# A transformer layer with attention and gated LoRA experts: activations transposed by VectorE and DRAM in place of TensorE, an earlier first product, and a plan whose transfers share one line

## The chip, the cores and the metric

The kernel runs on one core of one Trainium2 chip. The metric is the device time of one execution in microseconds (us), median of several runs, less being better.

## The reference

The input is x with 8 batches of 256 rows of 512 numbers, float32. All of it stays in float32.

```python
xn = (x - mean(x)) / sqrt(var(x) + 1e-5)               # per row
q, k, v = xn @ wq.T, xn @ wk.T, xn @ wv.T              # 32, 8 and 8 heads of 128
q, k = rope(q), rope(k)
scores = q @ k.T / sqrt(128)                           # 4 query heads share one key head
scores = scores * key_scale                            # 0.5 / 1.5 / 1.0 by key; rows from 107 on
probs = softmax(scores + causal_mask)
s = concat(probs @ v) @ wo.T
logits = xn @ router_w.T                               # 4 experts, the best 2 are kept
gates = softmax(top2(logits))
delta = sum_e gates_e * (xn @ A_e.T @ B_e.T) * 4       # rank 16
out = x + s * silu(delta)
```

## The kernel before

**Work and its parts.** Batches are taken in four pairs (`tb` 0 to 3), 512 rows or four tiles of 128 rows each. `norm(tb)` loads x, normalises it and puts the transposed activations into a tile `XB`; sums of its quarters go into `XT`. Both stand in a single buffer, so that a pair's `XB` can be written only when the last product of the pair before has read it.

All large products are done by Strassen's scheme with seven block products in place of eight. `quad` makes one projection of two times 256 output columns for a pair: `p1` and `p2` use parts of `XB`, `p6`, `p5`, `p7` and `p4` sums from `XT`, and `p3` `XB` again. Its PSUM banks are called `pa`, `pd` and `pe`, with a letter behind for queries, keys or values (`pak`, `pdq`). Each block product is eight matrix instructions of 128x256. The weight blocks and, from pair 1 on, their sums are fetched by GpSimd's queue into rings of nine and eight tiles; in pair 0 VectorE makes the sums and they are stored.

A step is one key head of a pair, `(tb, g)`; a unit is one batch of a step, so a step has two and the kernel 64, numbered 0 to 63. For each unit `softmax` computes scores (`sc`), exponentials and scaled probabilities; VectorE transposes them in blocks of 32 by 32 into `blocks`; SyncE stores them to DRAM with four transfers (`spread`, `there<-blocks`) and loads them with one (`gather`, `pT<-there`) in the order in which `values` needs them (`av<-pT,v`). `values` of a unit comes a step after its scores. `out_project` multiplies by the output weights and adds up seven sums in `acc` tiles. `put_together` combines them at the end of a pair, multiplies by the gates (`g`) and adds x (`xf`), which it loads with `inputs(0)` and `inputs(1)` into the two x buffers, 512 KB each, and stores the output. The last pair has its own version, `last_products`. `experts` computes router and gates from `XB` with `ra`, `bt` and `tab`.

**What sets the order.** A planner, `Plan`, runs through the whole kernel when it is built. Every piece of work is a job with an engine, an estimated time `takes`, jobs that it waits for (`after`), buffers that it opens and closes, and a `lag`: the time after its end until those behind it may start. TensorE's jobs get due times in the order in which they are laid; `run` derives the others' due times backwards from them, and then plays the kernel forward. Whenever an engine is free, the job due first, of those that are ready in that play, is issued. The instructions of each engine are put into the program in this order, and on the chip an engine keeps to it whatever the real durations are. A dependency that exists only in the plan makes an order, not a wait on the chip.

A transfer is a job whose `lag` is fixed: 6.0 us for a block of weights, 3.4 for the probabilities' stores behind 2.4 of issue, 7.0 for their gather behind 0.35 of issue, with `HOP` (0.18) for each step. Transfers do not hold each other up in the plan.

**The parts that the change touches.** In `norm`, for each tile: `load`, `statistics`, `variance`, `root`, `invert`, `normalise`, then `turn` (four TensorE transposes into a PSUM bank, `xp<-ident,xn`) and `read` (a copy by ACT into `XB`). The first pair's four turns are laid before the first products, `lay(norm(0))`, and its tables are loaded by `load_tables` on ACT's queue as one of the first jobs, beside the loads of x. From pair 1 on, the turns are laid between other products at the end of the step with g = 6.

Of the kernel before, what the change touches and what calls it, by code (L numbers as in the profile page):

```python
# [159 lines left out]
class Job:  # L160
# [3 lines left out]
    def __init__(self, engine, takes, what, after, opens, closes, near, lag, number):  # L164
        self.engine, self.takes, self.what, self.lag = engine, takes, what, lag
        self.opens, self.closes, self.near, self.number = opens, closes, near, number
        self.due, self.waits, self.then, self.started = float("inf"), len(after), [], False


class Plan:  # L170
# [4 lines left out]
    HOP = 0.18  # L175
    AHEAD = 30.0
# [4 lines left out]
    def add(self, engine, takes, what, after=(), opens=(), closes=(), near=None, lag=0.0):  # L181
        after = [a for a in after if a]
        job = Job(engine, takes, what, after, opens, closes, near, lag, len(self.jobs))
        for a in after:
            a.then.append(job)
        for hold in closes:
            hold.readers += 1
        self.jobs.append(job)
        return job

# [4 lines left out]
    def run(self):  # L195
        for job in reversed(self.jobs):
            if job.engine != "pe":
                if job.near:
                    job.due = job.near[0].due + job.near[0].takes + job.near[1]
                for after in job.then:  # L200
                    job.due = min(job.due, after.due - job.takes - job.lag - self.HOP)
        ready = {e: [] for e in ("pe", "dve", "act", "sp", "pool", "dma")}
        busy = dict.fromkeys(ready, 0.0)
        events, count = [], 0

        def offer(job):
            heapq.heappush(ready[job.engine], (job.due, job.number, job))

        for job in self.jobs:
            if not job.waits:  # L210
                offer(job)
        now, left = 0.0, len(self.jobs)
        laid = sorted((j for j in self.jobs if j.engine == "pe"), key=lambda j: -j.due)
        while left:
            while laid and laid[-1].started:
                laid.pop()
            limit = (laid[-1].due if laid else float("inf")) + self.AHEAD
            for engine, heap in ready.items():
                while heap and busy[engine] <= now:
                    tried, job = [], None  # L220
                    while heap:
                        entry = heapq.heappop(heap)
                        if entry[0] > limit:
                            tried.append(entry)
                            break
                        if all(h.room.has_for(h) for h in entry[2].opens):
                            job = entry[2]
                            break
                        tried.append(entry)
                    for entry in tried:  # L230
                        heapq.heappush(heap, entry)
                    if job is None:
                        break
                    for h in job.opens:
                        h.room.take()
                    job.started = True
                    job.what()
                    busy[engine] = now + job.takes
                    count += 1
                    heapq.heappush(events, (now + job.takes + self.HOP + job.lag, count, job))  # L240
                    heapq.heappush(events, (now + job.takes, -count, None))
            now, _, job = heapq.heappop(events)
            if job is None:
                continue
            left -= 1
            for h in job.closes:
                h.readers -= 1
                if not h.readers:
                    h.room.free += 1
            for after in job.then:  # L250
                after.waits -= 1
                if not after.waits:
                    offer(after)
# [3 lines left out]
def layer(ctx: ExitStack, tc: tile.TileContext, x, wquad, woquad, raT, bT, table, out):  # L257
# [14 lines left out]
    bounce = pool("bounce", 4, space=DRAM)  # L272
    store = pool("store", 1, space=DRAM)
# [31 lines left out]
    gates, sums_of, acts, weights, x_hold = {}, {}, {}, {}, {}  # L305
# [3 lines left out]
    def norm(tb):  # L309


        n = f"{tb}"
# [3 lines left out]
        ph = [hold("mm") for _ in range(NT)]  # L316
# [36 lines left out]

        def read(t):
            if t == 0:
                acts[tb] = (
                    one.tile([P, 2, NB, 2, S], F32, tag="XB", name=f"XB{tb}"),
                    one.tile([P, 4, 2, S], F32, tag="XT", name=f"XT{tb}"),
                )
            nc.scalar.copy(acts[tb][0][:, :, t // 2, :, bass.ts(t % 2, P)], box["p", t])  # L360

        def add_up(i):
            XB, XT = acts[tb]
            b11, b12, b21, b22 = XB[:, 0, 0], XB[:, 0, 1], XB[:, 1, 0], XB[:, 1, 1]
# [6 lines left out]
        for t in range(NT):  # L371
# [5 lines left out]
            add("dma", 0.0, lambda: None, after=[issues[t]], lag=8.5 if tb else 5.0 + 1.3 * t)  # L377
            for t in range(NT)
        ]
        sts = [add("dve", 0.9, lambda t=t: statistics(t), after=[loads[t]]) for t in range(NT)]  # L380
        begun.extend(issues)
        done = []

        for ts in [slice(0, NT)] if tb else [slice(t, t + 1) for t in range(NT)]:
            v = add("dve", 0.1, lambda ts=ts: variance(ts), after=sts[ts])
            r = add("act", 2.8 if tb else 0.2, lambda ts=ts: root(ts), after=[v])
            done += [add("dve", 0.1, lambda ts=ts: invert(ts), after=[r])] * len(sts[ts])
        reads, pieces = [], []
        for t in range(NT):
            xn = add("dve", 0.4, lambda t=t: normalise(t), after=[done[t]], opens=[mh[t]], closes=[xh[t // 2]])  # L390
            tp = add("pe", 0.5, lambda t=t: turn(t), after=[xn, identity], opens=[ph[t]], closes=[mh[t]])
# [11 lines left out]
        acts[tb, "B"], acts[tb, "T"] = reads, [t1, t2, t3, t4]  # L403
        return pieces
# [3 lines left out]
    def blocks_of(tb, room, ring, source, kept, key, form, first):  # L408
# [4 lines left out]
        order = (A11, A21, A22, A12, S1, S2, S4) if not tb else form.order  # L413
# [21 lines left out]
        if tb:  # L435
            for i in order:
                after = [sums_of[room, key, i]] if i in form.sums else []
                there[i] = add("pool", 0.8, lambda i=i: load(i), after=after, opens=[holds[i]], lag=6.0)
            return box, holds, there
        issue = list(first)  # L440
        for i in order[:4]:
            there[i] = add(
                "sp" if first else "pool", 0.4 if first else 0.8, lambda i=i: load(i), after=issue,
                opens=[holds[i]], lag=10.0 if first else 6.0,
# [6 lines left out]
        for i in form.sums:  # L451
            sums_of[room, key, i] = add(
                "pool", 0.8, lambda i=i: keep_sum(i), after=[there[i]], closes=[holds[i]],
                lag=5.0,
# [31 lines left out]
    def quad(tb, which, out, room, rows, name):  # L486
# [15 lines left out]
        def product(bank, i, half, b, t, first):  # L502
# [3 lines left out]
            xb = acts[tb][0][:, half, b] if t is None else acts[tb][1][:, t]  # L506
# [11 lines left out]
        def piece(bank, i, half, b, t, first, after):  # L518
            return add(
                "pe", 1.73, lambda: product(bank, i, half, b, t, first),  # L520
                after=[there[i]] + (XB if t is None else [XT[t]]) + after,
# [47 lines left out]
    def rope(src, of, dst, opens, after, name):  # L569
# [21 lines left out]
        def turn():  # L591
# [6 lines left out]
            after=after + [tables], opens=opens, closes=[of],  # L598
# [80 lines left out]
    free_p = [None]  # L679

    def softmax(tb, g, b):
# [119 lines left out]
        out_ = add("sp", 2.4, spread, after=[t1], closes=[bh], near=(sc, 5.0), lag=3.4)  # L801
        in_ = add("sp", 0.35, gather, after=[out_], opens=[th], lag=7.0)
# [116 lines left out]
    def last_products(n, abox, ah, a_done, wbox, wh, w_done):  # L919
# [18 lines left out]
        def load(what, b):  # L938
# [9 lines left out]
            loads[what, b] = add("sp", 0.3, work, after=after, opens=[hold(tag)], lag=9.0)  # L948
# [46 lines left out]
        def store(src, b, f, p, after, ts=slice(0, 2)):  # L995
# [3 lines left out]
                near=(p, 3.0), lag=4.0,  # L999
# [60 lines left out]
    def put_together(tb):  # L1060
# [15 lines left out]
        def inputs(b):  # L1076
# [4 lines left out]
            def load(what):  # L1081
# [4 lines left out]
            near = (M[2]["last"], -12.0)  # L1086
            done = [
                add("sp", 0.3, lambda: load("g"), after=gates[tb][2 * b : 2 * b + 2], opens=[xh],
                    near=near, lag=9.0),
                add("sp", 0.3, lambda: load("xf"), opens=[gh], near=near, lag=9.0),  # L1090
            ]
            loads[b] = box, [xh, gh], done

        def result(k, b, f):
# [17 lines left out]
                closes=[M[k]["hold"]], near=(near, 5.0), lag=4.0,  # L1112
# [18 lines left out]
    def experts(tb):  # L1131
# [5 lines left out]
        def route():  # L1137
            XB = acts[tb][0]
            lm = box["lm"] = ps_av.tile([P, NT, E + E * R], F32, tag="av", name=f"lm{n}")
            for t in range(NT):  # L1140
                for c in range(DC):
                    nc.tensor.matmul(
                        lm[:, t, :],
                        lhsT=XB[:, c // 2, t // 2, c % 2, bass.ts(t % 2, P)],
                        rhs=ra[:, c, :],
                        start=(c == 0),
                        stop=(c == DC - 1),
                    )
# [49 lines left out]
        p1 = add("pe", 3.75, route, after=acts[tb, "B"] + [tables], opens=[lh], closes=[x_hold[tb]])  # L1198
        r1 = add("dve", 2.0, rank_them, after=[p1], near=(p1, 2.0))
# [8 lines left out]
        def silu(t):  # L1208
# [15 lines left out]
            def whole():  # L1224
# [10 lines left out]
                    after=[d], closes=[h], near=(p, 4.0), lag=4.0,  # L1235
# [5 lines left out]
        return [p1], [p2], [[silu(t)] for t in range(NT)]  # L1241
# [41 lines left out]
    def load_tables():  # L1283
        nc.scalar.dma_start(out=tab, in_=table)
        nc.scalar.dma_start(out=ra, in_=raT.rearrange("(c p) m -> p c m", p=P))
        nc.scalar.dma_start(out=bt, in_=bT)

    identity = add("pool", 1.5, lambda: make_identity(tc.nc, ident), near=None)
    tables = add("act", 2.0, load_tables, lag=4.0)
# [8 lines left out]
    lay(norm(0))  # L1298
# [5 lines left out]
    lay(lead[:7] + route + lead[7:14] + turn + lead[14:])  # L1304

    for n in range(len(steps) + 2):
# [8 lines left out]
        if not last:  # L1315
# [7 lines left out]
            if tb + 1 < NTB and g == KV - 2:  # L1323
                turns = norm(tb + 1)
                for t in range(NT):
                    later[t] = later[t] + [turns[t]]
# [50 lines left out]
```

## Time and profile before

| | us |
|---|---|
| median of three runs | 1361.68 (1357.97, 1361.68, 1362.44) |
| profiled execution, its own time | 1358.35 |
| its span, first to last instruction | 1356.6 |
| TensorE busy | 1330.6 |
| VectorE busy | 1097.6 |
| ScalarE (ACT) busy | 618.5 |
| first large product starts | 14.02 |
| TensorE's waits for gathered probabilities | 9.4 in 6 waits |

The granted TensorE clock is 0.998 of full speed over the span. The DMA engines move 203 GB/s on average and are busy for 66% of the span. A line of a timeline has the start in us, the time in us, the engine, the line, the operation, out<-in by the program's names, and in brackets the idle time before and what ended it; a line of a list of waits has the total in us, how many times, and the longest. All instructions are recorded in a helper at line 118, so that they are told apart by their tiles. A q behind an engine's name is its queue of issues.

### The profile page before, as it was taken

The numbers are of one execution on the slowest core, as the hardware profiler recorded it, in microseconds if no ns is written. First come the engines' busy times: TensorE is split into PE (matmuls) and PEld (weight loads), VectorE is DVE, ScalarE is ACT, GpSimd is POOL, SyncE is SP. The second block draws the span as 40 slices with busy tenths as digits, with TensorE's granted clock in tenths as the row PEclk, the third lists the DMA queues.
The fourth block names the chain that finished last, engine by engine and source line by source line (L and its number), as shares of the span: only waits on it lengthen the run. The fifth ranks groups of instructions, "written<-read, shape, count | busy, mean of one in ns | idle before, by whom it ended". The sixth has DMA issues, their size and how long they took to land.

```text
span 1356.6 us, 19913 instructions
## 1 busy us (share of the span) xinstructions
PE 1330.6 (98%) x6512; PEld 1170.4 (86%) x6512; DVE 1097.6 (81%) x2827; ACT 618.5 (46%) x1590; POOL 314.1 (23%) x579
## 2 busy tenths in 40 slices
PE   7999999999999999999999999999999999999997
PEld 6888888888888888888888888888888988888986
DVE  5899989898888769689697875959868877676996
ACT  2465454453534435345453444435443455434621
POOL 2323222222222122221222122222122221222020
PEclk9999999999999999999999999999999999999999
DMA  5578766666766666676766666576676676565583
GB/s 172 180 250 256 216 186 223 217 212 207 242 177 212 207 197 185 202 226 181 215 200 217 200 213 202 171 226 206 178 227 193 197 219 202 188 198 186 156 282 106
DMA packets 106150, 275.81 MB, mean 203 GB/s; under 512 B 16000, under 2 KB 52864, under 8 KB 106048
## 3 DMA queue, kind: packets, MB, share of 16 engines
q0 software_dynamic: 45760, 149.98, 35.6%
q1 hardware_dynamic: 59536, 123.76, 29.9%
q8 instruction: 53, 0.87, 0.2%
q10 hardware_dynamic: 752, 0.80, 0.2%
q14 instruction: 49, 0.40, 0.1%
HBM read 194.79 MB, written 79.69 MB: 202 GB/s over the span
## 4 chain that ended last, share of the span: by engine, by line
PE 83%; DVE 9%; DMA 6%; issue 1%; ACT 1%; SPq 0%; DVEq 0%; ACTq 0%
PE po L118 23%; PE paq L118 14%; PE av L118 10%; PE sc L118 8%; PE pdq L118 7%; PE pak L118 4%; DMA pT<-there 4%; PE pav L118 4%; PE peq L118 3%; PE pdk L118 2%; DMA there<-blocks 2%; PE pdv L118 2%; DVE qTq L118 1%; DVE blocks L118 1%; DVE p L118 1%; DVE acc L118 1%
## 5 line engine op out<-in xcount | busy, mean ns | idle before, releaser
L118 ACT ACTIVATE p<-z,least 128x256 f32<-128x256 f32 (+7 forms) x512 | 207.6, 407 | 184.5 <-DVE least L118 137.0
L118 PE MATMUL po<-wo,a 128*128 128x256 f32 x992 | 233.3, 379 | 0.0
L118 PEld LDWEIGHTS po<-wo,a 128*128 128x128 f32 x992 | 186.4, 190 | 22.8
L118 PE MATMUL av<-pT,v 128*128 128x256 f32 x768 | 186.9, 383 | 9.4 <-DMA pT<-there 9.4
L118 DVE CUSTOM_DVE_ANT_0 z<-sc,tab 128x256 f32<-128x256 f32 (+7 forms) x512 | 134.0, 300 | 62.7 <-PE sc L118 59.3
L118 PE MATMUL paq<-XT,w 128*128 128x256 f32 x768 | 182.1, 380 | 0.3 <-ACT u3q L118 0.3
L118 PE MATMUL po<-wo,s 128*128 128x256 f32 x744 | 177.4, 381 | 0.2 <-PE av L118 0.2
L118 PEld LDWEIGHTS av<-pT,v 128*128 128x128 f32 x768 | 145.8, 192 | 30.8 <-issue 5.3
L118 PEld LDWEIGHTS sc<-kk,qTq 128*128 128x128 f32 x1024 | 159.0, 191 | 12.5 <-issue 0.8
L118 PE MATMUL sc<-kk,qTq 128*128 128x256 f32 (+7 forms) x1024 | 167.9, 302 | 0.1
L118 PEld LDWEIGHTS paq<-XT,w 128*128 128x128 f32 x768 | 144.9, 190 | 20.4 <-ACT u2q L118 0.8
L118 DVE TENSOR_TENSOR acc<-acc,po 128x512 f32<-128x512 f32 x189 | 128.2, 679 | 40.5 <-PE po L118 39.1
L118 POOL DMA_DIRECT2D w<-sums x144 | 78.9, 548 | 352.9 <-PE paq L118 158.7
L118 PEld LDWEIGHTS po<-wo,s 128*128 128x128 f32 x744 | 139.6, 190 | 23.7 <-issue 5.5
L118 ACT COPY a<-av 128x512 f32<-128x512 f32 x128 | 74.2, 580 | 179.6 <-PE av L118 179.2
L118 ACT COPY swq<-cq 64x1024 f32<-64x1024 f32 x128 | 133.7, 1045 | 15.0 <-DVE cq L118 10.7
L118 POOL DMA_DIRECT2D w<-in_wquad_dram x148 | 80.9, 548 | 244.9 <-PE paq L118 82.8
L118 DVE STREAM_TRANSPOSE blocks<-p 128x1024 f32<-128x1024 f32 (+1 forms) x128 | 123.6, 968 | 0.2
L118 DVE TENSOR_SCALAR p<-p,total 128x256 f32<-128x256 f32 (+7 forms) x512 | 117.1, 294 | 2.3
L118 DVE TENSOR_TENSOR qTq<-cq,tab 128x1024 f32<-128x1024 f32 x64 | 78.1, 1220 | 30.6 <-ACT cq L118 30.6
L118 ACT ACTIVATION_READ_ACCUMULATOR p<-z,least 128x1 f32 x512 | 95.8, 187 | 0.0
L118 POOL DMA_DIRECT2D wo<-in_woquad_dram x104 | 56.9, 548 | 128.4 <-PE po L118 118.5
(134 smaller groups left out, 1862.3 us busy)
## 6 DMA issues: line engine op xcount, KB each, us to landing
there<-blocks SPq DMA_DIRECT2D x256, 192.0 KB, 3.7
pT<-there SPq DMA_DIRECT2D x64, 768.0 KB, 5.9
w<-in_wquad_dram POOLq DMA_DIRECT2D x148, 256.0 KB, 4.5
w<-sums POOLq DMA_DIRECT2D x144, 256.0 KB, 4.0
wo<-in_woquad_dram POOLq DMA_DIRECT2D x104, 256.0 KB, 5.1
wo<-osums POOLq DMA_DIRECT2D x96, 256.0 KB, 5.0
sums<-w POOLq DMA_DIRECT2D x48, 256.0 KB, 4.2
osums<-wo POOLq DMA_DIRECT2D x32, 256.0 KB, 4.3
```

The lines of the kernel that those rows point to most:

```text
L118: ins = what(*args, **kwargs)
```

## The change

1. From pair 1 on, tiles are no longer transposed on TensorE. VectorE turns blocks of 32 by 32 (`turn_blocks`) into the x tile's own buffer, SyncE stores each half (two tiles) to DRAM with four transfers (`spread`) and loads it into `XB` with four (`gather`).
2. At the start the tiles are normalised two by two, the first product is laid behind the turns of two tiles, and products on `XB` wait in the plan only for the half that they read, for which `XB`'s dimensions are swapped. The first quads' weights come in the order of use. `tab` and `bt` are loaded behind the first read, `ra` on SyncE's queue behind x.
3. The plan gets one line for transfers: a job with `mb` megabytes takes its place on it at 0.38 MB per us, and has landed 3.3 us after.
4. `inputs` orders its loads behind stores of probabilities: the first two behind units 15 and 16 of the first pair (and their like later), the other two each behind the next step's first unit. They are due 25 us before a product in place of 12.
5. The router's products are split into one job for each tile.

```diff
+    RATE, LATENCY = 0.38, 3.3
...
+    def then(self, before, job):
+        before.then.append(job)
+        job.waits += 1
...
-                    busy[engine] = now + job.takes
+                    busy[engine] = there = now + job.takes
+                    if job.mb:
+
+                        wire = max(wire, now + 0.3) + job.mb / self.RATE
+                        there = max(there, wire + self.LATENCY)
+                    else:
+                        there += job.lag
                     count += 1
-                    heapq.heappush(events, (now + job.takes + self.HOP + job.lag, count, job))
+                    heapq.heappush(events, (there + self.HOP, count, job))
...
+        def turn_blocks(t):
+
+            to = xs["x", t // 2].rearrange("p t d -> p (t d)")
+            nc.vector.transpose(
+                to.rearrange("p (q k t s) -> p t k q s", q=NQ, k=DC, t=2)[:, t % 2],
+                box[t].rearrange("p (k q s) -> p k q s", q=NQ, s=BLK),
+            )
+
+        def spread(b):
+            there = box["there", b] = turned.tile(
+                [NQ, BLK, NQ, 2 * P], F32, tag=f"turned{b}", name=f"turned{tb}_{b}"
+            )
+            for a in range(NQ):
+                nc.sync.dma_start(
+                    out=there[:, :, a, :].rearrange("q r e -> r q e"),
+                    in_=xs["x", b][bass.ts(a, BLK)]
+                    .rearrange("r t d -> r (t d)").rearrange("r (q e) -> r q e", q=NQ),
                 )
...
+        def gather(b):
+            if b == 0:
+                new_acts()
+            to = acts[tb][0][:, b].rearrange("p h c (t a s) -> p a (h c t) s", t=2, a=NQ)
+            for a in range(NQ):
+                nc.sync.dma_start(
+                    out=to[:, a],
+                    in_=box["there", b][:, :, a, :].rearrange("q r (k s) -> (q r) k s", s=BLK),
+                )
...
+        if tb:
+            for b in range(NB):
+                turns = [
+                    add("dve", 0.6, lambda t=t: turn_blocks(t), after=xn[2 * b : 2 * b + 2], closes=[mh[t], xh[b]])
+                    for t in (2 * b, 2 * b + 1)
+                ]
+                out_ = add("sp", 2.4, lambda b=b: spread(b), after=turns, closes=[xh[b]], lag=3.4, mb=0.5)
+                reads += [
+                    add("sp", 2.4, lambda b=b: gather(b), after=[out_] + reads[:1],
+                        opens=[] if b else [x_hold[tb]], lag=7.0, mb=1.0)
+                ] * 2
+        for t in [] if tb else range(NT):
+            tp = add("pe", 0.5, lambda t=t: turn(t), after=[xn[t], identity], opens=[ph[t]], closes=[mh[t]])
...
-                there[i] = add("pool", 0.8, lambda i=i: load(i), after=after, opens=[holds[i]], lag=6.0)
+                there[i] = add("pool", 0.8, lambda i=i: load(i), after=after, opens=[holds[i]], lag=6.0, mb=0.25)
...
-                after=[there[i]] + (XB if t is None else [XT[t]]) + after,
+                after=[there[i]] + (XB[2 * b : 2 * b + 2] if t is None else [XT[t]]) + after,
...
-        out_ = add("sp", 2.4, spread, after=[t1], closes=[bh], near=(sc, 5.0), lag=3.4)
-        in_ = add("sp", 0.35, gather, after=[out_], opens=[th], lag=7.0)
+        out_ = add("sp", 2.4, spread, after=[t1], closes=[bh], near=(sc, 5.0), lag=3.4, mb=0.75)
+        spreads.append(out_)
+        if behind and len(spreads) % 2:
+            plan.then(out_, behind.pop(0))
+        in_ = add("sp", 0.35, gather, after=[out_], opens=[th], lag=7.0, mb=0.75)
...
-            near = (M[2]["last"], -12.0)
+            near = (M[2]["last"], -25.0)
...
+            if b == 0:
+                plan.then(spreads[-3], done[0])
+                plan.then(spreads[-2], done[1])
+            else:
+                behind.extend(done)
...
-    lay(norm(0))
+
+    tiles = norm(0)
...
-    lay(lead[:7] + route + lead[7:14] + turn + lead[14:])
+    lay(tiles[:2] + lead[:1] + tiles[2:] + lead[1:7] + route + lead[7:14] + turn + lead[14:])
```

## The prediction

> **What bounds the kernel now.** I read the page's first part, then who waited for whom on TensorE, then the timeline at the start, at the turn from one batch pair to the next, and of SyncE.
>
> ```profile
> PE 1330.6 (98%) x6512; PEld 1170.4 (86%) x6512; DVE 1097.6 (81%) x2827; ACT 618.5 (46%) x1590; POOL 314.1 (23%) x579
> ```
>
> TensorE is the bound: of the span's 1356.6 us only 26.0 are idle. A gain must remove TensorE work or come out of these 26. Its waits:
>
> ```profile
> PE av L118 <- DMA pT<-there: 9.4, 6, 2.4
> PE xp L118 <- DVE rstd L118: 8.9, 2, 8.5
> PE xp L118 <- DVE xn L118: 0.9, 2, 0.8
> ```
>
> 9.4 us are six waits of `values` for gathered probabilities (in six of 64 units), 9.8 are the start, 0.5 others, and 6.2 the tail after the last product, which the change leaves. Nothing waits for weights. The start, and the first turn of batch pairs:
>
> ```profile
> 13.11 1.12 PE L118 MATMUL xp<-ident,xn 128*128 128x128 f32 x4 [0.17 <-DVE xn L118]
> 14.02 3.59 PE L118 MATMUL pak<-XB,w 128*128 128x256 f32 x8
> 17.43 1.90 PE L118 MATMUL pek<-XB,w 128*128 128x256 f32 x8
> 19.17 1.89 PE L118 MATMUL pak<-XT,w 128*128 128x256 f32 x8
> ...
> 287.58 1.89 PE L118 MATMUL pdq<-XB,w 128*128 128x256 f32 x8
> ...
> 291.71 0.60 PE L118 MATMUL xp<-ident,xn 128*128 128x128 f32 x4
> 292.14 1.89 PE L118 MATMUL po<-wo,a 128*128 128x256 f32 x8
> ...
> 301.72 1.97 PE L118 MATMUL pak<-XB,w 128*128 128x256 f32 x8
> ...
> 307.80 1.89 PE L118 MATMUL pak<-XT,w 128*128 128x256 f32 x8
> ```
>
> A product takes 1.73 us from start to start (3.41 at 14.02, on a clock not yet warm), and a turn of one tile 292.14 - 291.71 = 0.43. The last product on the old XB is issued by 289.31, the first on the new starts at 301.72, the first on XT at 307.80. SyncE, around a gather that is late:
>
> ```profile
> 423.62 2.30 SPq L118 DMA_DIRECT2D there<-blocks  x4
> 429.23 0.34 SPq L118 DMA_DIRECT2D g<-gates  x1
> 430.41 0.34 SPq L118 DMA_DIRECT2D pT<-there  x1
> 430.79 0.43 SPq L118 DMA_DIRECT2D xf<-in_x_dram  x1
> ```
>
> Here a 512 KB load is issued ahead of the gather, another and a store just behind; the gather lands 8.3 us after issue (median 5.9) and TensorE waits 1.02 us at 438.87. The same place waits 1.41 us at 771 and 2.44 at 1104.
>
> **Turns of batch pairs 1 to 3.** 12 tile turns leave TensorE: 12 x 0.43 = 5.2 us, all on the path, since no wait stands there. By the weight loads (141 ns, 48 of them) it would be 6.8; I take the starts. ACT loses 12 copies (7.0 us), which it waited for anyway. VectorE gets 12 block transposes at 0.70 (row of the 128x512 stream transposes): 8.4 us, 2.8 per turn. It is 92 to 94% busy in 262 to 301, 595 to 634 and 927 to 966, but 72 to 88% in the 38 us before, and normalising falls due some 15 us earlier (the plan counts 2.4 + 7.0 + 0.18 for each of two gathers in a row and 6.0 for the stores); I cost it at nothing. Without that cover the 2.8 us would delay probabilities, whose tight units have under 1 us.
>
> SyncE gets 16 issues per turn. The stores are done before the old XB is free; the gathers (4 issues, 2.3 us by the four-store row) start at 289.31 and must serve products at 301.72 and 307.80, each 1.76 earlier without the turns: 10.65 and 16.7 us later. A half is 4 x 128 x 8 = 4096 pieces of 128 B. The trace's packet records have 272 B at 19 ns (the 512 of the `ra` load, starting at best 16 in 25 ns), 1024 B at 46, 4 B at 9. At 19 to 25 ns over 16 engines a half takes 4.9 to 6.4 us, and with 3.2 fixed (the 192 KB stores land in 3.7, of which 0.5 is packets) the first is there after 8.1 to 9.6: in time. The second, directly behind, ends at 13.0 to 16.0, plus two subtractions of 0.68: 14.4 to 17.4 against 16.7. Nothing to 0.7 late, three times; I take 0.6 in all, near the low end, since 128 B lies between the 9 and 19 ns rows. While SyncE waits for the old XB, only the second half and unit 12's stores (297.72) are queued behind.
>
> The row speaks for short pieces; the Trainium skill, DMA: Bandwidth & Descriptors, Specifications, speaks against: it asks for at least 512 B for line rate and has the engine read, modify and write below it. If that doubled each piece's time to 38 ns, its sum would be that of the second rival; the 272 B row, also under 512 B, shows no such step.
>
> **The start.** Tables no longer share the line with x: the first tile's statistics start at 5.60, while the shortest x load lands 4.1 us after issue (0.75): 4.85 or a little less. Then two statistics (0.87 each), root and reciprocal (0.65), normalising (0.5 each), turn and copy (about 2.0 by the same steps at 8.52 to 10.23) put the first product near 10 in place of 14.02. It runs 3.4 us cold; turns 2 and 3 follow (0.9 to 1.7), then their copies (0.6) and two subtractions (1.4) before a product on XT, with pek in between. That product's loads start at 16.2 to 17.7 in place of 18.96. I take a gain of 2.4, bounds 1.2 to 2.8. `tab` and `ra` land well before the rank at 28.07, their first use.
>
> **The plan's new arrivals.** Old: a unit's probabilities are promised 2.4 + 3.4 + 0.18 + 0.35 + 7.0 + 0.18 = 13.5 us after the first store's issue. New: 2 x (0.3 + 0.75/0.38 + 3.3 + 0.18) = 11.5, plus whatever is on the line. In the trace the 32 units first in their step take 12.6 on average, 9.2 to 16.6, and TensorE takes most of them as soon as promised, on average 0.8 later (a piece in progress). Summing max(0, real - promise - 0.8) over them (unit 60 left out, slack 9.8) gives 10.1 us for the old promise, where 9.4 was measured: the rule holds. Applying the new one to the trace's issue times, all transfers on one line, gives 18.8: on average it promises 1.5 us earlier. Of that, 6.2 falls on units 14, 30 and 46, where both 512 KB loads stand right behind the gather (341.73, 342.60 behind 341.35; it lands in 8.9 us). The change puts these loads behind stores, where the line is idle while the stores' landing is awaited. So 12.6, net +2.5. Bounds: -4.9 (the three waits at 439, 771 and 1104 gone, nothing else) to +14.7 (18.8 in full, +8.7, plus 2 us each at units 8, 24 and 40, beside which the earlier x loads now fall, unpriced on the plan's line). The second pair of loads gains little at 439: `g` still waits for an x buffer that VectorE frees at 429.2, and still goes ahead of the gather; only xf moves. Weights are promised at 4.4 instead of 7.0 (real 4.0 to 5.1) but prefetched a ring ahead: nothing; if that cover went, 0.7 us a load. The last results of a pair come some 40 us later; six of the seven sums they share rooms with are free by then: nothing, or one TensorE bank held.
>
> **Sum.** -5.2 - 2.4 + 2.5 + 0.6 = -4.5. On the profiled execution's own time (1358.35, span 1356.6 and 1.8 around it): 1353.9. The three runs' median is 1361.68, 3.3 above that execution; carried over: 1357.2, say 1357.
>
> **Rivals.** *Promises too early, slower*: at `values` behind units 2, 8, 24, 40, 62 and the like TensorE waits more than it saves. Price: +14.7 in place of +2.5, so +7.7: 1369.4. It decides from waits for probabilities over 9.4 + 7.0 = 16.4 us. For it: the 18.8 above; against: the loads that caused 6.2 of it move.
> *128-byte pieces slow, slower*: at 38 ns a half takes 9.8 us, the second ends at 22.8 + 1.4 = 24.2, 7.5 late, three times: +22, 1379. It decides from 23.6 ns a piece, (16.7 - 1.4 - 3.2)/2 x 16/4096. Against it: the 272 B row.
> *Most of it cancels, same*: `g` waits for its buffer as before so units 18, 34, 50 keep their waits, the start gives 1.2, the probabilities cost +5: -5.2 - 1.2 + 5 = -1.4, 1360.3. For it: the buffer's wait shown above.
>
> **How the numbers follow.** About 0.3% (4.1 us) is what a measurement of this kernel can tell from no change. Forecast 0.50, of which 0.42 beyond 4.1 us (its own range 1350 to 1360); cancelling 0.24; early promises 0.18; slow pieces 0.08. Faster 0.42; same 0.24 + 0.08 = 0.32; slower 0.18 + 0.08 = 0.26. Faster and slower cases together hold most, so the range reaches from 1350 (-5.2 - 2.4 - 4.9 = -12.5, nearly) to 1370, the early promises' price; slow pieces and the extreme gain are left out.
>
> **What would show it.** Right: 16 `xp` products in place of 64; first `pak` near 10; waits of `av` for `pT` near 12 us; no wait of `pak` for XB at the turns; g and xf issued between `there` and `pT`. Wrong: `pak` or `pek` waiting for DMA XB at 300, 632 and 964; waits for `pT` over 16 us; a first product after 12 us; new waits of TensorE for weights, VectorE or banks, of which I have none.

## The result

The changed kernel takes 1354.26 us (median of 20 runs, 1350.25 to 1360.43), the kernel before 1359.70 (20 runs, 1353.85 to 1362.80): ratio 0.9966, interval 0.9952 to 0.9980, so 4.6 us or 0.34% faster. Its profiled execution took 1353.95 us (span 1352.2) beside 1358.35 (1356.6). Foretold were 1357.0 for the median and 1353.9 for the profiled execution.

The page's engine line and TensorE's waits (total us, times, longest) of the changed kernel:

```profile
PE 1326.2 (98%) x6464; PEld 1167.3 (86%) x6464; DVE 1106.1 (82%) x2835; ACT 611.2 (45%) x1576; POOL 315.2 (23%) x579
```

```profile
PE av L118 <- DMA pT<-there: 9.9, 3, 5.8
PE xp L118 <- DVE xn L118: 7.4, 2, 6.5
PE po L118 <- DVE s L118: 0.9, 1, 0.9
PE pak L118 <- ACT XB L118: 0.7, 1, 0.7
PE pak L118 <- issue: 0.4, 1, 0.4
```

48 transposes have left TensorE. The waits for probabilities have not become less (9.4 us before), but three take the place of six, and one is 5.8 us long. TensorE's timeline at the start, at unit 2, at the first turn of pairs (with unit 12) and at unit 16:

```profile
6.54 1.94 PE L118 MATMUL xp<-ident,xn 128*128 128x128 f32 x8 [6.54 <-DVE xn L118]
9.16 3.78 PE L118 MATMUL pak<-XB,w 128*128 128x256 f32 x8 [0.68 <-ACT XB L118]
16.35 0.65 PE L118 MATMUL xp<-ident,xn 128*128 128x128 f32 x4 [0.83 <-DVE xn L118]
...
111.15 1.19 PE L118 MATMUL av<-pT,v 128*128 128x256 f32 x2 [5.80 <-DMA pT<-there]
...
303.01 1.97 PE L118 MATMUL pak<-XB,w 128*128 128x256 f32 x8
...
309.64 1.97 PE L118 MATMUL pak<-XT,w 128*128 128x256 f32 x8 [0.39 <-issue]
...
317.86 4.32 PE L118 MATMUL av<-pT,v 128*128 128x256 f32 x12 [2.80 <-DMA pT<-there]
...
403.49 1.53 PE L118 MATMUL av<-pT,v 128*128 128x256 f32 x6 [1.27 <-DMA pT<-there]
```

The first product starts at 9.16 in place of 14.02. At the turn no product on the new XB waits for it. The next `values`, unit 12's, waits 2.80 us. SyncE's timeline of the same kernel (start, us of issuing) shows what stands ahead of it and, in the last three lines, unit 18:

```profile
281.44 6.50 SPq L118 DMA_DIRECT2D turned<-x  x8
288.03 0.41 SPq L118 DMA_DIRECT2D pT<-there  x1
292.58 10.24 SPq L118 DMA_DIRECT2D XB<-turned  x8
302.92 3.85 SPq L118 DMA_DIRECT2D there<-blocks  x4
312.10 0.34 SPq L118 DMA_DIRECT2D pT<-there  x1
...
430.35 2.23 SPq L118 DMA_DIRECT2D there<-blocks  x4
437.39 0.34 SPq L118 DMA_DIRECT2D pT<-there  x1
437.77 0.43 SPq L118 DMA_DIRECT2D g<-gates  x1
```

The eight gathers of XB keep SyncE for 10.24 us, and unit 12's stores come directly behind. VectorE had the last of what they store ready at 302.07:

```profile
301.36 0.71 DVE L118 STREAM_TRANSPOSE blocks<-p 128x512 f32<-128x512 f32 x1
```

So the queue held the first store up for only 0.85 us. The larger part is in the stores themselves: they take 3.85 us to issue and 9.0 to land, where the kernel before has 2.2 and 6.3 for the same unit.

At unit 18 the gather of probabilities now stands ahead of `g`, which stood ahead of it before, and so it is at units 34 and 50. The waits at 439, 771 and 1104 are gone.

To compare traces I add up TensorE's time as start of its first instruction + instructions at their usual pitch (from start to start) + excess over that pitch (waits, and stretches on a slow clock) + the tail. The start gives 8.52 to 6.54 = -2.0; the pitch 48 x 0.109 = -5.2; the excess 26.6 to 28.9 = +2.3; the tail 6.3 to 6.9 = +0.6. Together -4.3, where the spans differ by 4.4. The excess by stretches of each kernel's own time:

| us | 0-40 | 40-125 | 125-290 | 290-330 | 330-400 | 400-900 | 900-1300 | 1300-1340 | sum |
|---|---|---|---|---|---|---|---|---|---|
| before | 5.5 | 3.2 | 1.6 | 0.2 | 0.9 | 5.5 | 5.0 | 4.6 | 26.6 |
| after | 5.2 | 9.1 | 0.9 | 5.3 | 0.2 | 4.4 | 2.4 | 1.2 | 28.9 |

What the three old waits and the end gave, unit 2 (40 to 125) and the first turn (290 to 330) took.

### The profile page after: what moved, and what is told of

Same layout as the page of the kernel before. It is cut to its first block, busy times and chain, and to the rows that moved or that the text cites. A ratio compares the mean times of both kernels' runs of the same rounds, so it can differ in the third digit from the quotient of the medians.

```text
span 1352.2 us, 19913 instructions
## 1 busy us (share of the span) xinstructions
PE 1326.2 (98%) x6464; PEld 1167.3 (86%) x6464; DVE 1106.1 (82%) x2835; ACT 611.2 (45%) x1576; POOL 315.2 (23%) x579
## 4 chain that ended last, share of the span: by engine, by line
PE 83%; DVE 11%; DMA 4%; issue 1%; SPq 1%; ACT 0%; DVEq 0%; ACTq 0%
PE po L118 24%; PE paq L118 14%; PE av L118 10%; PE sc L118 8%; PE pdq L118 7%; PE pak L118 4%; PE pav L118 4%; PE peq L118 4%; DMA there<-blocks 2%; PE pdk L118 2%; PE pdv L118 2%; DMA pT<-there 2%; DVE blocks L118 2%; DVE p L118 2%; DVE acc L118 1%; DVE z L118 1%
```

## The experiments

My theory after the result: the turns and the start gave what they were priced at, and the line takes much of both back, by promising probabilities too early. The rival: the line is worth little either way, and what is lost is lost to the 128-byte pieces. That the start gives more than its 2.4, by way of SyncE's order at units 18, 34 and 50, I took up only after the run of the start alone. A percentage of 0.1 is 1.36 us; of a difference between two experiments the uncertainty is 0.2 to 0.3%.

**The change without the line.** Jobs keep their fixed lags.

```diff
-                    if job.mb:
+                    if False and job.mb:
```

> The change with the old fixed lags in place of the shared line (mb is ignored); turns, start and moved loads stay. Theory (the line promises probabilities 1 to 1.5 us too early, which costs 2.5 us of waits net of what the moved loads give back): faster than the change by 1 to 4 us, waits of av for pT 5 to 9 us. Rival (the line is what holds the waits at 9.9 us although loads now stand behind the stores): slower than the change by 3 us or more, waits of 13 us or more.

Measured: 1348.12 us, ratio 0.9919 (0.9896 to 0.9941). Waits for `pT` 8.7 us, but seven with 2.8 as the longest, and unit 2's among them fell from 5.8 to 2.8. The line costs the change 0.47%, 6.4 us, more than the whole change gains and more than the 1 to 4 us that the theory asked for (3.5 between the two spans).

**The change with the turns on TensorE.**

```diff
-        if tb:
+        if False:
...
-        for t in [] if tb else range(NT):
+        for t in range(NT):
...
-                norm(tb + 1)
+                turns = norm(tb + 1)
+                for t in range(NT):
+                    later[t] = later[t] + [turns[t]]
```

> The change with all pairs' tiles turned on TensorE again. Theory (48 transposes at 0.109 us are on the path, and the detour over DRAM costs TensorE a wait at the first turn only): 64 xp products, TensorE's products sum to 5.2 us more; no wait of 2.8 us at the first turn of pairs, so 1 to 5 us slower than the change. Rival (what VectorE and SyncE pay for the detour eats the turns' 5.2 us): same time as the change within 1 us or faster.

Measured: 1358.93 us, ratio 0.9995 (0.9978 to 1.0011). So the turns by VectorE and DRAM bring 0.29% (0.9995 to 0.9966), 3.9 us of the 5.2 that they take from TensorE. At the first turn there is no excess here (0.2 us in 290 to 330, 5.3 with the change): the 2.80 us wait of unit 12 belongs to the turn's transfers.

**The change with the loads of g and xf as before.** Due 12 us ahead again, behind no store.

```diff
-            near = (M[2]["last"], -25.0)
+            near = (M[2]["last"], -12.0)
...
-            if b == 0:
-                plan.then(spreads[-3], done[0])
-                plan.then(spreads[-2], done[1])
-            else:
-                behind.extend(done)
```

> The change with the loads of g and xf ordered as in the kernel before (due 12 us ahead, not behind stores). Theory (the moved loads take the delay from the units whose gather they stood beside): waits of av for pT rise by 3 to 7 us, at the units 14, 30, 46 or 18, 34, 50, and it is 3 to 7 us slower than the change. Rival (the line accounts for the loads wherever they stand, the move is worth nothing): within 1.5 us of the change.

Measured: 1356.25 us, ratio 0.9979 (0.9964 to 0.9994), six waits for `pT` with 11.1 us together. Moving the loads brings 0.13% (1.8 us), which is within the uncertainty; the 3 to 7 us of the theory did not come.

**A later promise.** Each transfer on the line is reckoned to land 4.3 us after its place in place of 3.3.

```diff
-    RATE, LATENCY = 0.38, 3.3
+    RATE, LATENCY = 0.38, 4.3
```

> The change with a latency of 4.3 in place of 3.3 us on the plan's line: a unit's probabilities are promised 2.0 us later. Theory (a product for which TensorE waits was put too early by the promise, and there is other work to do first): waits of av for pT fall from 9.9 to 2 to 6 us, 3 to 7 us faster than the change. Rival (the large waits, 5.8 at unit 2 and 2.8 at unit 12, come from SyncE's queue and a crowded line that another 2 us do not cover, or other orders bring new ones): waits of 8 us or more, within 2 us of the change.

Measured: 1345.36 us, ratio 0.9898 (0.9876 to 0.9921): 0.68% less than the change by one number, more than the theory asked for. TensorE's waits:

```profile
PE xp L118 <- DVE xn L118: 8.1, 2, 6.6
PE av L118 <- DMA pT<-there: 3.3, 1, 3.3
PE pak L118 <- DMA XB<-turned: 2.8, 1, 2.8
```

Two of the three waits for probabilities are gone, unit 2's is 3.3 in place of 5.8, and with less waiting elsewhere the XB gathers become late at the first turn.

**The start alone.** The three edits above of the line, the turns and the loads in one kernel. What is left of the change is the start and the router's split products.

> Only the start of the change: all pairs turned on TensorE, old fixed lags, loads of g and xf as before. Theory (the start is worth 2.2 us, nothing else moves): 64 xp products, waits of av for pT about 9 us as before, 1 to 4 us faster than the kernel before. Rival (moving the first products shifts the tight units and costs as much in waits): within 1 us of the kernel before.

Measured: 1349.09 us, ratio 0.9945 (0.9932 to 0.9959), 7.5 us faster than before; in the profiles 9.8 (span 1346.8). TensorE's first instruction starts 1.85 us earlier, and up to 40 us the excess differs by 0.1: the start itself gives some 2.0. The theory that nothing else moves fell. The rest is later: the excess of 400 to 600 falls from 2.5 to 1.3, of 600 to 900 from 3.0 to 1.4, of 1100 to 1300 from 4.1 to 1.6, of 1300 to 1340 from 4.6 to 1.9. SyncE's timeline of this kernel at unit 18 has the gather ahead of `g`:

```profile
421.55 2.23 SPq L118 DMA_DIRECT2D there<-blocks  x4
428.11 0.34 SPq L118 DMA_DIRECT2D pT<-there  x1
428.49 0.43 SPq L118 DMA_DIRECT2D g<-gates  x1
```

So the order flipped without any edit to the loads: the plan's new times were enough.

**The start and the line.** As the last one, but with `if job.mb:`.

> The start and the shared line on top of it, TensorE's turns and the loads as before. Theory (the line is what costs: it promises too early): 4 to 9 us slower than the start alone, so 1 to 6 us slower than the kernel before, waits of av for pT 13 us or more. Rival (the line only costs together with the gathers over DRAM or the moved loads): within 2 us of the start alone.

Measured: 1359.08 us, ratio 1.0014 (1.0002 to 1.0026). The line by itself costs 0.69%, 9.4 us (12.2 between the two spans), though waits for `pT` rose only from 3.7 to 8.1 us and not to 13. TensorE's timeline of this kernel at unit 2 and at the longest of a new kind of wait:

```profile
111.84 1.62 PE L118 MATMUL av<-pT,v 128*128 128x256 f32 x3 [6.08 <-DMA pT<-there]
...
459.47 2.00 PE L118 MATMUL paq<-XT,w 128*128 128x256 f32 x8 [2.13 <-ACT u3q L118]
```

and SyncE's ahead of unit 2:

```profile
92.89 2.39 SPq L118 DMA_DIRECT2D there<-blocks  x4
102.13 0.34 SPq L118 DMA_DIRECT2D pT<-there  x1
```

The stores land after 9.2 us and the gather after 9.6; in the start alone it is 6.8 and 9.1, and 9.6 for the gather in the kernel before. So the stores are what became slower. Five of GpSimd's transfers of 256 KB are issued among them, from 92.54 to 94.81; in the start alone the last of these five is issued 2.4 us ahead of the first store. That they are the cause is likely but was not tested. The DMA engines as a whole are no busier (77% from 90 to 113 against 87%). TensorE comes to the product 12.9 us behind the first store in place of 14.3. Of the 4.2 us that the wait grew, 1.4 are this earlier promise and 2.8 the later arrival. Of the excess of 30.4 against 18.6, waits of `av` take 4.6, of `paq` 3.3, and slow-clock pitches 4.3.

**The turn's gathers in runs of 1 KB.** The change with each row loaded as 1024 bytes in place of eight pieces of 128; XB's bytes lie in another order, so that only the time counts.

```diff
-            to = acts[tb][0][:, b].rearrange("p h c (t a s) -> p a (h c t) s", t=2, a=NQ)
+            to = acts[tb][0][:, b].rearrange("p h c s -> p (h c s)")
...
-                    out=to[:, a],
-                    in_=box["there", b][:, :, a, :].rearrange("q r (k s) -> (q r) k s", s=BLK),
+                    out=to[:, bass.ts(a, 2 * P)],
+                    in_=box["there", b][:, :, a, :].rearrange("q r e -> (q r) e"),
```

> The change, with the gathers' pieces of 128 B replaced by whole runs of 1 KB, so that XB is filled with the right bytes in the wrong places; same bytes, same number of issues. Theory (the pieces' price is SyncE's queue: eight issues take 8 to 10 us in place of 4 to 5, and unit 12's stores stand behind them): eight issues in 4 to 6 us, the 2.8 us wait at unit 12 gone with its slower clock, 2 to 5 us faster than the change in the profile. Rival (unit 12 waits for its stores because VectorE and the line are full there): issues shorter, but the wait at unit 12 stays within 1 us of 2.8.

Measured: 1349.21 us, ratio 0.9947 (0.9933 to 0.9961). SyncE's timeline of it at the first turn:

```profile
291.63 4.59 SPq L118 DMA_DIRECT2D XB<-turned  x8
301.14 2.61 SPq L118 DMA_DIRECT2D there<-blocks  x4
```

The same bytes in longer runs take SyncE 4.59 us in place of 10.24, unit 12's stores are issued as soon as VectorE is done and land after 5.3 us in place of 9.0, and the wait of 2.80 us is gone (excess of 290 to 330: 0.2). The short pieces cost 0.19% or some 2.6 us, at the limit of what can be told apart. This run does not show how much of that is the queue's: the changed kernel's 24,576 records of 128 bytes take 13 ns each, 6.7 us of the 16 engines' time for one turn, and its share in records of 1 KB at 46 ns takes 2.9.

**A later promise, and the gathers' issue at its measured length.** Theory: the wait for XB of 2.8 us goes when the plan knows how long SyncE is kept.

```diff
-    RATE, LATENCY = 0.38, 3.3
+    RATE, LATENCY = 0.38, 4.3
...
-                    add("sp", 2.4, lambda b=b: gather(b), after=[out_] + reads[:1],
+                    add("sp", 5.1, lambda b=b: gather(b), after=[out_] + reads[:1],
```

> The later promise (latency 4.3) and XB's gathers planned at 5.1 us of SyncE's time each in place of 2.4, as measured. Theory (the plan lays the first products of a pair where XB is not there yet, since it thinks SyncE done after 2.4): the 2.8 us wait of pak for XB of the later promise goes, 2 to 5 us faster than with the later promise alone. Rival (the wait is a crowded line, not the queue; other work is not there to be laid in front): same time within 1 us and a wait at the same place.

Measured: 1348.19 us, ratio 0.9928 (0.9912 to 0.9945), no better than the later promise alone (0.9898). `pak` still waits 2.7 us for XB. That theory fell.

**Still later.** As the last one, with 5.3 for the landing.

> The change with the landing of every transfer reckoned at 5.3 us in place of 3.3, and 5.1 us in place of 2.4 for SyncE's issue of four gathers of XB. Theory, that early promises are what the line costs: waits for pT fall under 3 us (at 3.3 they were 9.9, at 4.3 they were 3.3), but the plan lays more in front of values and the turn's order is the plan's only; 1344 to 1348, ratio about 0.990. Rival, that a promise of over 4.3 is later than the chip and costs elsewhere (banks or buffers held longer): over 1350, ratio over 0.994.

Measured: 1339.78 us, ratio 0.9867 (0.9847 to 0.9886), the fastest of all. TensorE's waits, and its timeline at unit 2:

```profile
PE xp L118 <- DVE xn L118: 7.4, 2, 6.7
PE pak L118 <- DMA XB<-turned: 1.1, 1, 1.1
PE av L118 <- DMA pT<-there: 0.9, 1, 0.9
```

```profile
110.91 2.83 PE L118 MATMUL av<-pT,v 128*128 128x256 f32 x12 [0.87 <-DMA pT<-there]
```

One number, 4.3 to 5.3, brings 0.61%, more than the theory asked for; beside the run with 4.3 alone (0.9898) it is 0.31%, at the limit of what can be told apart. By the sum of the prediction a unit's probabilities are promised after 2 x (0.3 + 0.75/0.38 + landing + 0.18): 11.5 us at 3.3, 13.5 at 4.3, 15.5 at 5.3. All of these are for an empty line. Of the 32 units first in their step, 24 take over 11.5 in the changed kernel, 11 over 13.5 at 4.3, and 2 over 15.5 here. Promises that few units miss cost nothing that the trace shows: the excess falls from 28.9 to 15.9.

**Start and turns, no line, loads as before.**

> The change without the line and with the loads of g and xf as before: the earlier start and the turns by VectorE and DRAM alone. Start alone had a span of 1346.8. Theory, that turns are worth their 48 transposes whatever the plan (-5.2) less what the 128-byte pieces hold up on SyncE (1 to 3 us at the first turn): 1342.5 to 1345, ratio about 0.990. Rival, that SyncE's queue gives all of it back at the three turns: 1346 to 1349, ratio 0.992 to 0.995, with waits of av for pT over 5 us near 313, 640 and 975.

Measured: 1346.72 us, ratio 0.9916 (0.9899 to 0.9933), span 1343.1, within the theory's range; no wait for `pT` is over 2.2 us. Beside the start alone (0.9945) the turns bring 0.29%, the third agreement after 0.29% above and 0.35% between the two kernels with the line and the loads as before (1.0014 to 0.9979).

**The order alone.** The kernel before, with `g` of the second half ordered behind the gather of unit 18, 34 and 50. In `softmax`, behind the gather's job:

```diff
+        if behind:
+            job = behind.pop()
+            in_.then.append(job)
+            job.waits += 1
```

and `inputs(1)` puts its `g` into `behind`.

> The kernel before with one order changed: g of a pair's second half is ordered in the plan behind the gather of unit 18, 34 and 50, which it went ahead of. Theory, that the earlier start alone shortened the kernel by 9.8 us chiefly because this order flipped there: the three waits of av for pT at 439, 771 and 1104 (1.02, 1.41 and 2.44 us, 4.9 in all) go and the slow clock behind later waits with some of them; pT waits fall from 9.4 to about 4.5 us; the first product stays at 14.0; the span falls by 4 to 6 us from 1356.6, to about 1351, ratio about 0.996. Rival, that the flip was only beside the gain: the span stays within 1.5 us, ratio 0.999 to 1.001, and the waits stand elsewhere.

Measured: 1353.89 us, ratio 0.9964 (0.9950 to 0.9979); in the profiles only 2.3. TensorE's timeline:

```profile
114.35 4.51 PE L118 MATMUL av<-pT,v 128*128 128x256 f32 x12 [2.20 <-DMA pT<-there]
...
772.18 1.61 PE L118 MATMUL av<-pT,v 128*128 128x256 f32 x6 [2.11 <-DMA pT<-there]
```

The waits at 439 and 1104 are gone; the one near 771 stays, since there the gather was issued only 9.1 us after the stores (755.84 to 764.90), whatever the order behind it. Unit 34's stores take 9.0 us to land, here and in the kernel before; in the twelve kernels with the earlier start they take 6.5 to 6.9. In the kernel before, all three gathers leave 0.1 us behind the landing of their stores, so that `g` ahead of them did not hold up their issue. It can only have slowed the transfers.

Of the start's 0.55% the order by itself gives 0.36% in the medians, which is for the theory, though the span fell by less than it asked for; 0.19%, 2.6 us, remain for the start itself. The traces support this only in part. The stretches with units 18 and 50 give 3.6 us of excess, but another 2.7 are gained behind 1300, where no load was moved, and the wait near 771 and unit 2 take back 4.4. And the three gathers land after 7.0 to 7.1 us here, after 4.4, 4.4 and 5.8 in the start alone. The place of `g` is not all that the start changed there; GpSimd's weight loads, too, are issued at other times beside these gathers. Their part was not tested.

**The turn's gathers on GpSimd's queue.** With 4.3 for the landing:

```diff
-                nc.sync.dma_start(
+                nc.gpsimd.dma_start(
...
-                    add("sp", 2.4, lambda b=b: gather(b), after=[out_] + reads[:1],
+                    add("pool", 5.0, lambda b=b: gather(b), after=[out_] + reads[:1],
```

> The change with the landing of every transfer reckoned at 4.3 us in place of 3.3, and the eight gathers of XB of a turn issued by GpSimd's queue in place of SyncE's. With SyncE's queue the later promise alone left a wait of pak for XB of 2.8 us at 300 and one for pT of 3.3 us at unit 2, span 1346.0. Theory, that SyncE's issue of the short pieces is what is late at the turn: the wait for XB goes, 1341 to 1344, ratio about 0.987. Rival, that the pieces themselves or GpSimd's issue take as long: the wait for XB stays near 2.8 or weights come late, 1346 to 1352, ratio 0.990 to 0.994.

Measured: 1344.71 us, ratio 0.9896 (0.9879 to 0.9914), against 0.9898 from SyncE: the same, though the wait for XB is gone, so the time that the theory asked for did not come. GpSimd's timeline of it at the first turn:

```profile
290.44 3.54 POOL L118 DMA_DIRECT2D XB<-turned  x4 [2.10 <-issue]
293.97 0.57 POOL L118 DMA_DIRECT2D osums<-wo  x1
```

GpSimd issues four in 3.5 us and weights queue behind them. With the same pieces and the same promise, unit 12's stores leave SyncE at once when VectorE is done (299.70 behind 299.68); with SyncE issuing the pieces they leave 4.5 us later than that (303.37 behind 298.91). So the hold-up in the queue is shown, but not that it decides the time. Unit 2 still waits 3.5 us; that one is not the turn's.

## Why the prediction was right, and where it was not

The time and the sign were right, and two terms behind them were wrong, in opposite directions. That -4.6 stands beside the foretold -4.5 is therefore luck. Along one chain of kernels, by ratios:

| step | ratio after it | us | foretold |
|---|---|---|---|
| earlier start | 0.9945 | -7.5 | -2.4 |
| turns off TensorE, with their transfers | 0.9916 | -3.9 | -5.2 + 0.6 |
| loads behind stores | 0.9919 | +0.4 | part of +2.5 |
| one line | 0.9966 | +6.4 | part of +2.5 |
| all | | -4.6 | -4.5 |

**Turns: right.** The transposes were worth what was foretold (12 x 0.43 against 48 x 0.109), and VectorE's 12 block transposes took 0.69 each at no cost to be seen. The 0.6 for late gathers became 1.3 (3.9 gained of 5.2), and in another place: I looked for `pak` waiting for XB at the turns and found none. What was mis-sized is SyncE's issue. I took 2.3 us for four gathers from the row of the four stores of probabilities, and the eight took 10.2, 8.0 and 8.5 at the three turns. Unit 12's stores, which I named as queued behind, paid, not the second half of XB: 0.85 us by starting later, the rest by a slower issue and landing.

**128-byte pieces: cheaper on the engines than foretold.** They took 13 ns a piece against a forecast of 19 to 25, so the second rival's 23.6 was never near. The 25 rested on 16 of the `ra` load's pieces starting in 25 ns at best; the trace has 16 starts within 17 ns. The Trainium skill, DMA: Bandwidth & Descriptors, Specifications, has the engine read, modify and write below 512 B; no step of that kind shows in 13 ns for 128 B beside 19 for 272 in the kernel before.

**The start: right in itself, wrong in what it set off.** The first product came at 9.16 (near 10 foretold), and the first instruction with the excess up to 40 us gives 2.0 + 0.3 = 2.3 of the foretold 2.4 (the 0.3 is no more than kernels with the same start differ by, 4.7 to 5.6). The failed step is "g still waits for an x buffer that VectorE frees at 429.2, and still goes ahead of the gather". In all eight kernels with the earlier start and either no line or a landing of 3.3, the gather goes first at unit 18; in the four with 4.3 or 5.3, `g` is ahead again by some 0.5 us, and there `values` has slack. How much of the -7.5 comes by this order is shown only in part, as said above. I held an order of the old plan fixed while moving the times that it was made from; the -4.9 stood in the text as a bound of another term.

**The plan's new arrivals: sign right, size wrong.** +2.5 was foretold with the moved loads, and the two steps gave +6.8 here, +9.4 with the line alone on top of the start; the bound of +14.7 holds. Two things were missed. First, I applied the new promise to stores and gathers at the old issue times and landings. In the first pair the new plan brings unit 2's scores and stores forward, 96.92 to 92.89 between the two start kernels, in among GpSimd's transfers, and the stores land after 9.2 us in place of 6.8. The 2.8 us by which unit 2's probabilities take longer were in no row of before; the earlier promise itself is 1.4 of the 6.08 us of waiting. Second, I priced only waits for probabilities; the slower clock behind a wait and the waits of `paq` for ACT's `u3q` came on top. That waits for `pT` in the changed kernel are 9.9 and not the 12 foretold is then no support: they lack the three that the order took away.

**The first rival** (promises too early) names what does decide here: with the start alone it makes the kernel no faster than before, 1.0014. It did not come out on top because the start paid for it. The third rival rested on the buffer's wait at units 18, 34 and 50, and falls with it.

What stays open: whether a line is better than fixed lags at the same lateness. At one lateness two runs can be compared: fixed lags and the line with 4.3 both promise probabilities after 13.5 us, if the line is empty, and take 0.9919 and 0.9898. The line then has waits for `pT` of 3.3 us in place of 8.7, but the ratios are not told apart. The latest promise with the line (0.9867) beats the fixed lags, but fixed lags with a later promise were not run. Nor is it settled why unit 34's stores land so late, which is what holds up the gather near 765.

## What to carry to other kernels

When a plan made before the run orders the queues, a promise that is too early costs a wait on the bounding engine, while one 2 us later cost nothing that showed here (later ones were not run); so reckon transfers with the slow ones of the trace, not with the mean. An order taken from the old trace may be relied on only if the edit moves neither of the two times that made it. Price a transfer of short pieces on the queue that issues it as well as on the DMA engines, and look for who stands behind it there.

## What the hardware did that I had not expected

A wait of TensorE costs more than itself when it falls into one window of its clock. The granted clock in the traces changes on a grid of 3.41 us. These are windows of that grid: us from and to, busy time of each engine, granted clock, DMA share and GB/s; first of the kernel before, around the waits of 2.12 us at 1324 and of 2.44 us at 1104, then of the changed kernel at unit 2:

```profile
1321.35:1324.75 3.40, 1.28 (x7) 0.83 (x6) 2.12 (x4) 0.00 (x0) 0.56 (x1) 1.00 0.94 334
1324.75:1328.16 3.41, 3.41 (x10) 2.69 (x9) 0.00 (x0) 0.58 (x1) 0.00 (x0) 0.50 0.22 87
1099.40:1102.80 3.40, 2.36 (x11) 1.71 (x10) 3.37 (x13) 1.09 (x3) 0.74 (x2) 1.00 1.00 391
1102.80:1106.20 3.40, 2.00 (x10) 1.82 (x11) 1.96 (x4) 0.43 (x1) 0.34 (x1) 1.00 0.95 348
```

```profile
105.81:109.23 3.42, 0.00 (x0) 0.00 (x0) 2.51 (x7) 0.17 (x1) 0.39 (x1) 1.00 0.95 368
109.23:112.64 3.41, 1.49 (x4) 1.25 (x5) 0.00 (x0) 0.00 (x0) 0.00 (x0) 0.50 0.18 68
112.64:116.05 3.41, 3.41 (x10) 2.80 (x9) 0.36 (x3) 0.00 (x0) 0.00 (x0) 0.50 0.00 0
```

The wait of 2.12 us lies within one window, and the next runs at 0.50 with 10 of TensorE's instructions, where most full windows at 1.00 have 17 or 18. The longer one is split over two windows, and both stay at 1.00. Over all 14 profiles, 16 windows at 1.00 had TensorE idle for 2.07 us or more, and each was followed by one at 0.50; 38 had 0.82 to 1.89, and the clock behind stayed at 1.00. Windows that are at 0.50 themselves need less: of 22, the six with 0.63 us idle or more were followed by another at 0.50, the 16 with 0.42 or less by one at 1.00. A window at half speed loses up to 1.7 us. The Trainium skill, TensorE: Matmul & The Clock Gate, Part 1, gives the same window of 3413 ns running on its own, and half speed after at least one idle window; these runs agree on the window, and show that some 61% of one idle (2.07 of 3.41) is enough.
